# An attention and expert layer on one core: a reordered opening, and maxima transposed half a step later

## The chip, the cores and the metric

The kernel runs on 1 core of one Trainium2 chip. The metric is the device time in microseconds (us) of one execution, median of the runs shown. Five engines run side by side, each with its own in-order queue: TensorE (PE; the profile lists its weight loads as PEld), VectorE (DVE), ScalarE (ACT), GpSimd (POOL) and SyncE (SP), which only issues DMAs. ACT and POOL issue DMAs too.

## The reference, cut to what matters

`x` has 4 sequences of 2048 tokens and 512 channels; all is float32.

```python
xn = layernorm(x)
# attention: 16 heads of 32
q, k, v = split(xn @ w_qkv)                    # w_qkv: 512 x 1536
q, k = irfft(rfft(q) * sigmoid(mask_logits)), irfft(rfft(k) * sigmoid(mask_logits))   # in each head
attn = softmax(q @ k.T / sqrt(32))             # 2048 x 2048 for each head
a = concat_heads(attn @ v) @ w_out + b_out
# experts: the best of 8 for each token, 100 places in each expert, first come first served
best = argmax(softmax(xn @ w_gate))
f = gate * (xn @ w_expert + b_expert) for the tokens that have a place, else 0
out = x + a + f
```

## The kernel before, in words

**Filter.** The spectral filter of q and k is a 32 x 32 matrix for each head. It is folded into the weights: `filter_steps(c)` gives, for the column chunk c (128 columns, four heads) of the q weights (s = 0) and the k weights (s = 1), a step `turned` (four transposes on PE into a PSUM bank, a copy to SBUF) and a step `filtered` (four matmuls with the filter matrix `filt`, a copy, and for c > 0 a DMA into the DRAM scratch `wd[c]`). The unfiltered weights stand in `raw`. The filter matrix comes from the mask (`mask`, `freq`, a sigmoid on ACT, one matmul, `same_head`).

**Tokens.** `token_stage(b)` gives the steps of a sequence, for its 16 tiles of 128 tokens: `load`, `measure` (two statistics instructions on DVE), `scale` (on POOL, the last part on DVE where `shift_on` is given), `normalize` (ACT, or DVE with `fast`), `turn` (four transposes on PE, a copy on ACT into `xnT`).

**Head groups and blocks.** The work is 16 groups k (4 sequences x 4 chunks of four heads), each with 4 query blocks n of 512 queries. `projections(k)` gives the pieces that make queries, keys and values of a group; a piece covers 128 tokens (16 small matmuls and a copy on ACT), or 512 with `tiles = TQ`. `key_steps(n)` forms differences of neighbouring key tiles on POOL.

**Maxima.** The softmax needs the greatest score of each query and head before the exponentials. `stream` lists the items: 32 for each block (k, n). An item takes two matmuls (`max_matmuls`, array<-keys,q) into two of the eight PSUM banks, and a reduction of both on DVE (`max_reduce`, part<-array; one instruction of 128 x 1024 if the banks are neighbours, else two of 128 x 512). When the 32nd item of a block is reduced, the block goes to `full_blocks`; `max_negate` makes the negated maxima `neg` on DVE; `max_turn` transposes them on PE (array<-square,neg), either inside the next projection piece, in a spare part of its bank, or in a bank of its own; `max_store` copies them with ACT, `max_split` splits them into three bfloat16 rows on POOL and sends these with three DMAs to `negm`, which `shift` multiplies into the scores' banks at the start of a block.

**The main loop.** A half is one key tile j of a block: 16 halves make a block, two halves a window, 1024 halves the loop. A half holds two items of the maxima stream, the scores of the key tile (array<-q,steps_of_keys), two exponentials on ACT (even or odd <-array), the products with the values of the tile before (array<-even,v or odd,v) and their sum on DVE (num), and then the steps of its `agenda`. PE's queue is in program order, so what waits in a half holds all of PE's work behind it. `MAX_AHEAD` says how many items the stream is ahead of the loop: so many are done in the opening.

**The planner.** `plan(k)` fills the agenda. `spread` lays steps with a cost over the halves at the lowest even level at which all are placed in time; key pieces may come only after the old keys are spent (`after_keys_are_spent`, `SPENT`).

**Order.** `on.tensor`, `on.vector`, `on.scalar`, `on.gpsimd` are held in program order by `InOrder`. In the opening, DMAs on SP (`nc.sync`) are not held so; from the maxima on, `on.sync` is.

**The opening before** loads all q and k weights, then x; filters all four chunks; normalizes and turns the first four tiles; projects keys and queries of the first block in pieces of 512 columns; then takes 40 items one by one, with wide pieces at items 6, 14, 22, 28 and 33 and turns in between (`ahead`). `closing` puts a block's transposition two items after its negation. In the main loop the transposition follows the negation within the same half:

```python
while full_blocks:
    splits[window + 1] = full_blocks.pop(0)
    max_negate(*splits[window + 1])
    negated.append(splits[window + 1])
if left:
    products(*left)
...
for step in agenda[2 * window + (j == odd)]:
    step()
if negated:
    max_store(max_turn(bank(), 0))
```

Of the kernel before, what the change touches and what calls it, by code (L numbers as in the profile page):

```python
# [25 lines left out]
P = 128  # L26
# [16 lines left out]
MAX_AHEAD = 40  # L43
# [3 lines left out]
def shape_constants():  # L47
# [19 lines left out]
        "c_square": square.astype(np.float32),  # L67
        "c_falling": np.ascontiguousarray(falling, dtype=np.float32),
        "c_token": token.astype(np.float32),
# [34 lines left out]
def attention_and_top1_experts(ctx: ExitStack, tc: tile.TileContext, a: dict, out: bass.AP):  # L104
# [28 lines left out]

    mask = const.tile([2 * NF, 1], F32, name="mask")
# [5 lines left out]
    square = const.tile([P, 3, P], F32, name="square")  # L140
    nc.scalar.dma_start(out=square, in_=a["c_square"])
    ident, upto, same_head = (square[:, j, :] for j in range(3))
# [30 lines left out]
    wd = [dram1.tile([P, NR, 3, P], F32, name=f"wd{c}") for c in range(NG)]  # L173
    wg = {}
    raw = {}
    for s in range(2):
        both = probs(s == 1)
        for g in range(NR // 2):
            raw[s, g] = both[:, g]
            nc.sync.dma_start(out=raw[s, g], in_=w_qkv[:, 2 * g : 2 * g + 2, s * DM : (s + 1) * DM])  # L180
# [14 lines left out]
    def filter_steps(c):  # L195
# [3 lines left out]
        def turned(s):  # L199
            if s == 0:  # L200
                held["wt"] = probs(c % 2 == 1)
            pt = bank()
            for r in range(NR):
                on.tensor.transpose(
                    pt[:, r * P : (r + 1) * P], raw[s, r // 2][:, r % 2, c * P : (c + 1) * P], ident
                )
            on.vector.tensor_copy(held["wt"][:, s, 0, :], pt)
# [22 lines left out]
    def token_stage(b):  # L230
# [10 lines left out]
        def load_tile(i):  # L241
            n, t = divmod(i, TQ)
            if t == 0:
                held[n] = chunk("xs")
            on.sync.dma_start(out=held[n][:, t : t + 1, :], in_=x[b, n, :, t : t + 1, :])
# [163 lines left out]
    def load_qkv_weights(k, s):  # L409
        wg[k, s] = weights.tile([P, NR, P], F32, name=f"w{s}", bufs=1)  # L410
        on.sync.dma_start(out=wg[k, s], in_=wd[k % NG][:, :, s, :])
# [348 lines left out]
    load, measure, scale, normalize, turn, first_route, first_sums, _ = token_stage(0)  # L760

    load(0)
# [3 lines left out]
    for s in range(3):  # L766
        wg[0, s] = weights.tile([P, NR, P], F32, name=f"w{s}", bufs=1)
    nc.sync.dma_start(out=wg[0, 2], in_=w_qkv[:, :, 2 * DM : 2 * DM + P])
    for c in range(1, NG):
        cols = slice(2 * DM + c * P, 2 * DM + (c + 1) * P)  # L770
        nc.sync.dma_start(out=wd[c][:, :, 2, :], in_=w_qkv[:, :, cols])
    filters = [filter_steps(c) for c in range(NG)]
    turned, filtered = ([f[2 * s + i] for f in filters for s in range(2)] for i in range(2))
    for i in range(2 * NG + 1):
        if i < 2 * NG:
            turned[i]()
        if i > 0:
            filtered[i - 1]()
        if 2 * NG - TQ <= i < 2 * NG:
            measure(i - 2 * NG + TQ)  # L780
    for s in range(3):
        nc.sync.dma_start(out=wd[0][:, :, s, :], in_=wg[0, s])
    first_projections = projections(0, TQ)
# [4 lines left out]
    for i in range(TQ):  # L788
        measure(TQ + i)
    scale(TQ, 2 * TQ, on.vector)  # L790
    for i in range(TQ, 2 * TQ):
        normalize(i)
        measure(TQ + i)
    first_projections[0]()
    scale(2 * TQ, 3 * TQ, on.vector)
    for i in range(2 * TQ, 3 * TQ):
        if i == 3 * TQ - 1:
            first_projections[1]()
        normalize(i)
        measure(TQ + i)  # L800
    scale(3 * TQ, NT, on.vector)
    falling = const.tile([P, E], F32, name="falling")
    nc.scalar.dma_start(out=falling, in_=a["c_falling"])
    token = const.tile([P, NT], F32, name="token")
    nc.scalar.dma_start(out=token, in_=a["c_token"])

    w_gate = const.tile([P, NR, DH], F32, name="w_gate")
    nc.gpsimd.memset(w_gate, 0.0)
    nc.scalar.dma_start(out=w_gate[:, :, 0:E], in_=a["L0_ffn_w_gate"].rearrange("(r p) e -> p r e", p=P))
    b_out = const.tile([P, DM], F32, name="b_out")  # L810
    nc.scalar.dma_start(out=b_out, in_=a["L0_attn_b_out"].partition_broadcast(P))


# [5 lines left out]
    for table in tables:  # L819
        nc.sync.dma_start(out=table.rearrange("(t p) c -> p t c", p=P), in_=nobody)  # L820

    load_out_weights(0)

    ahead = {6: first_projections[2], 14: first_projections[3], 22: first_projections[4]}
    ahead.update({28: first_projections[5], 33: first_projections[6]})
    for i, item in ((4, 1), (8, 9), (12, 17)):
        ahead.update({item + 2 * j: lambda i=i + 2 * j: (turn(i), turn(i + 1)) for j in range(2)})
    ahead.update({4: lambda: normalize(12), 5: lambda: normalize(13)})
    ahead.update({7: lambda: normalize(14), 8: lambda: normalize(15)})
    first_projections = projections(0)[7 * TQ :]  # L830
    on.sync = InOrder(tc, nc.sync)
    key_steps(0)
    closing = {}
    for i, item in enumerate(stream[:MAX_AHEAD]):
        if i == 30:
# [3 lines left out]
        half = next(turns), next(turns)  # L839
        max_matmuls(item, half)  # L840
        max_reduce(item, half, False)
# [302 lines left out]
```

## Time and profile before

| | |
|---|---|
| median of 3 runs | 4225.1 us (4222.73 to 4227.74) |
| the profiled execution | 4220.07 us |
| its span, first to last instruction | 4218.3 us |
| busy: PE, DVE, POOL, ACT | 99%, 82%, 70%, 59% of the span |
| mean granted clock of PE | 0.998 |
| first item of the maxima on PE | 40.20 us |
| first shift matmul of the main loop | 99.14 us |
| DMA | 685.93 MB, mean 163 GB/s |

The engines' busy shares are of the whole span. PE's matmuls are pipelined and their ends are modelled, so a PE that is busy 99% need not run at its peak. Nearly all instructions carry line 84, that of the helper `InOrder`; groups are told apart by tile names. Four-byte matmuls show as two records each, transposes as one. The granted clock of PE is given as a share of full speed, by stretch.

### The profile page before, as it was taken

The page shows a single profiled execution, that of the slowest core. Times are in us where ns is not written, and L with a number is a line of the kernel's source. Part 1 is how long each engine was busy: PE and PEld are TensorE (multiplying, and loading weights), DVE is VectorE, ACT ScalarE, POOL GpSimd, SP SyncE. Part 2 cuts the span into 40 slices and gives each one's busy share as a digit, 9 for nine tenths or more (in the row PEclk, how much of TensorE's full clock was granted, in tenths as well). Part 3 has the DMA queues.
Part 4 walks back from the last instruction along what each step waited for, and adds up shares of the span by engine and source line. Part 5 has one row for each costly group of instructions (what it writes and reads, how often), then busy time and mean ns, then how long its engine had stood idle before and what let it go on. Part 6 is the DMA issues. An engine that isn't in the chain of part 4 may idle for free.

```text
span 4218.3 us, 120261 instructions
## 1 busy us (share of the span) xinstructions
PE 4166.4 (99%) x52270; PEld 1837.7 (44%) x52270; DVE 3440.0 (82%) x4962; ACT 2489.1 (59%) x3411; POOL 2968.4 (70%) x2046
## 2 busy tenths in 40 slices
PE   8999999999999999999999999999999999999998
PEld 4444444444444444444444444444444443444432
DVE  6778888987788888897788888888778888788896
ACT  3555556666565556657565556566656555556665
POOL 1567776776876767776687766767668776677873
PEclk9999999999999999999999999999999999999999
DMA  4667778997788778899677787899877976778788
GB/s 121 144 139 154 155 159 163 220 197 151 139 158 161 155 156 164 187 199 193 132 158 157 156 161 150 162 199 203 169 148 146 183 158 134 148 160 165 156 170 178
DMA packets 183416, 685.93 MB, mean 163 GB/s; under 512 B 26902, under 2 KB 56760, under 8 KB 117608
## 3 DMA queue, kind: packets, MB, share of 16 engines
q0 software_dynamic: 110432, 605.83, 73.5%
q1 hardware_dynamic: 71280, 71.90, 5.4%
q8 instruction: 409, 6.70, 0.6%
q14 instruction: 119, 0.97, 0.1%
q10 hardware_dynamic: 1176, 0.52, 0.1%
HBM read 71.85 MB, written 88.96 MB: 38 GB/s over the span
## 4 chain that ended last, share of the span: by engine, by line
PE 93%; DVE 5%; DMA 1%; issue 1%; ACT 0%; POOL 0%; SPq 0%; ACTq 0%; POOLq 0%; DVEq 0%
PE array L84 93%; DVE part L84 3%; DVE num L84 1%; DVE factor L84 0%; DMA even<-odd 0%; ACT odd L84 0%; DVE stats L84 0%; DMA w<-wd 0%; ACT even L84 0%; DMA odd<-in_L_attn_w_qkv_dram 0%; DVE even L84 0%; POOL rstd L84 0%; DVE neg L84 0%; DMA mask<-_L_attn_mask_logits_dram 0%; DVE mv L84 0%
## 5 line engine op out<-in xcount | busy, mean ns | idle before, releaser
L84 DVE TENSOR_REDUCE part<-array 128x1 f32<-128x512 f32 (+1 forms) x3132 | 2483.3, 848 | 681.0 <-PE array L84 678.0
L84 POOL TENSOR_TENSOR even<-even 128x1024 f32<-128x1024 f32 x876 | 2123.6, 2528 | 410.5 <-DMA even<-odd 406.5
L84 PE MATMUL array<-keys,q 32*128 32x512 f32 x8192 | 2066.0, 614 | 7.9 <-DVE num L84 2.9
L84 PE MATMUL array<-q,steps_of_keys 32*128 32x512 f32 x8192 | 2030.7, 616 | 2.4 <-issue 2.1
L84 ACT ACTIVATE odd<-array 128x1024 f32<-128x1024 f32 x1024 | 996.0, 1021 | 483.3 <-PE array L84 413.4
L84 ACT ACTIVATE even<-array 128x1024 f32<-128x1024 f32 x1024 | 994.2, 1021 | 447.6 <-PE array L84 434.8
L84 PEld LDWEIGHTS array<-keys,q 32*128 32x128 f32 x8192 | 776.9, 184 | 565.8 <-DVE part L84 351.1
L84 PEld LDWEIGHTS array<-q,steps_of_keys 32*128 32x128 f32 x8192 | 691.9, 184 | 274.6 <-issue 250.8
L84 POOL DMA_DIRECT2D even<-odd x510 | 464.8, 911 | 394.9 <-ACT odd L84 346.6
L84 DVE TENSOR_TENSOR num<-num,array 128x512 f32<-128x512 f32 x960 | 650.5, 678 | 23.5 <-PE array L84 23.4
L84 PEld LDWEIGHTS array<-xnT,w 128*32 128x32 f32 x15808 | 443.3, 110 | 264.0 <-DVE part L84 172.3
L84 PE MATMUL array<-even,v 128*32 128x512 f32 x4096 | 545.5, 605 | 1.0 <-DVE part L84 1.0
L84 PE MATMUL array<-odd,v 128*32 128x512 f32 x4096 | 545.9, 605 | 0.0
L84 PE MATMUL array<-xnT,w 128*32 128x128 f32 (+1 forms) x15808 | 525.2, 277 | 1.5 <-ACT xnT L84 0.7
L84 PEld LDWEIGHTS array<-w,xnT 128*32 128x32 f32 x8192 | 230.4, 110 | 146.8 <-DVE part L84 106.6
L84 DVE RECIPROCAL factor<-den 128x64 f32<-128x64 f32 x504 | 274.4, 545 | 0.0
L84 PE MATMUL array<-wo,ot 128*32 128x512 f32 x2048 | 267.0, 594 | 5.0 <-POOL ot L84 5.0
L84 PE MATMUL array<-w,xnT 128*32 128x128 f32 x8192 | 269.4, 273 | 1.3 <-DMA w<-wd 1.1
L84 PEld LDWEIGHTS array<-even,v 128*32 128x32 f32 x4096 | 80.6, 108 | 390.1 <-DVE part L84 381.2
L84 PEld LDWEIGHTS array<-odd,v 128*32 128x32 f32 x4096 | 80.8, 108 | 388.4 <-DVE part L84 379.9
L84 POOL DMA_DIRECT2D out_dram<-y x63 | 86.5, 1373 | 202.8 <-ACT y L84 125.6
L84 ACT COPY q<-array 128x128 f32<-128x128 f32 (+1 forms) x250 | 66.9, 268 | 186.1 <-PE array L84 182.3
(129 smaller groups left out, 1478.9 us busy)
## 6 DMA issues: line engine op xcount, KB each, us to landing
even<-odd POOLq DMA_DIRECT2D x510, 1024.0 KB, 8.4
out_dram<-y POOLq DMA_DIRECT2D x63, 1024.0 KB, 9.8
xs<-in_L_attn_x_dram SPq DMA_DIRECT2D x96, 256.0 KB
out_dram<-in_L_attn_x_dram SPq DMA_DIRECT2D x16, 1024.0 KB
w<-wd SPq DMA_DIRECT2D x45, 256.0 KB
wo<-in_L_attn_w_out_dram SPq DMA_DIRECT2D x16, 256.0 KB
negm<-row SPq DMA_DIRECT2D x192, 4.0 KB
xs<-in_L_attn_x_dram SPq DMA_DIRECT2D x2, 1024.0 KB
```

The lines of the kernel that those rows point to most:

```text
L84: done = act(*args, **kwargs)
```

## The change

- **Constants.** `falling` and `token` join `square` in one array, loaded first, on SP. `w_gate` and `b_out` are loaded on SP too, after x.
- **Loads.** Of the q and k weights, the first 128 columns of each are loaded first, then the first 512 tokens of x in two transfers, then the other columns, then the rest of x. `on.sync` is in order from here. The value weights are read from `w_qkv` itself, not from `wd`, which has two parts instead of three.
- **Order of the opening.** Chunk 0 is turned and filtered; four tiles measured; chunk 1 turned; four tiles normalized and turned; chunk 1 filtered; four tiles measured; five pieces of 128 tokens projected. Then 42 items follow in 21 pairs: both items' matmuls, both reductions, then the steps of `beside[p]`: turns, pieces of 128 tokens, the remaining measures and normalizations, chunks 2 and 3 (their `turned` copies on ACT), the key steps, and at pairs 14 to 17 one clearing of an expert table each, written in another layout.
- **Maxima.** `MAX_AHEAD` is 42. A negated block waits in `fresh` until the next half, where it is transposed.
- **Planner.** `spread` takes latest places, used for the key pieces: a step is not moved past its latest half to keep the level.

```diff
-MAX_AHEAD = 40
+MAX_AHEAD = 42
...
+    square = const.tile([P, 3 * P + E + NT], F32, name="square")
+    nc.sync.dma_start(out=square, in_=a["c_square"])
...
-    wd = [dram1.tile([P, NR, 3, P], F32, name=f"wd{c}") for c in range(NG)]
+    wd = [dram1.tile([P, NR, 2, P], F32, name=f"wd{c}") for c in range(NG)]
...
-        both = probs(s == 1)
-        for g in range(NR // 2):
-            raw[s, g] = both[:, g]
-            nc.sync.dma_start(out=raw[s, g], in_=w_qkv[:, 2 * g : 2 * g + 2, s * DM : (s + 1) * DM])
+        raw[s] = probs(s == 1).rearrange("p g r n -> p (g r) n")
+        nc.sync.dma_start(out=raw[s][:, :, 0:P], in_=w_qkv[:, :, s * DM : s * DM + P])
...
-            on.vector.tensor_copy(held["wt"][:, s, 0, :], pt)
+            copy = on.vector.tensor_copy if c < 2 else on.scalar.copy
+            copy(held["wt"][:, s, 0, :], pt)
...
-        on.sync.dma_start(out=wg[k, s], in_=wd[k % NG][:, :, s, :])
+        cols = slice(2 * DM + k % NG * P, 2 * DM + (k % NG + 1) * P)
+        on.sync.dma_start(out=wg[k, s], in_=w_qkv[:, :, cols] if s == 2 else wd[k % NG][:, :, s, :])
...
+    on.sync = InOrder(tc, nc.sync)
+    for i in range(0, TQ, 2):
+        load_tile(i, 2)
+    for s in range(2):
+        on.sync.dma_start(out=raw[s][:, :, P:], in_=w_qkv[:, :, s * DM + P : (s + 1) * DM])
     load(1)
     load(2, chunk("y"))
     load(3, probs(False).rearrange("p u h q -> p (u h) q"))
...
+    first_projections = projections(0)
...
+    for step in (*turned0, *filtered0):
+        step()
+    for i in range(TQ):
+        measure(i)
+    for step in turned1:
+        step()
     scale(0, TQ, on.vector)
     for i in range(TQ):
         normalize(i, fast=True)
         turn(i)
+    for step in filtered1:
+        step()
+    for i in range(TQ, 2 * TQ):
+        measure(i)
+    scale(TQ, 2 * TQ)
+    for i in range(TQ + 1):
+        project_first(i)
...
+    beside = {p: [] for p in range(MAX_AHEAD // 2)}
+    for p, pieces in enumerate(((5,), (6, 8), (7, 9), (10, 11), (12,), (13,), (14,), (15,), (16,), (17,), (18,), (19,))):
+        beside[p] += [lambda i=i: project_first(i) for i in pieces]
+    for i in range(TQ):
+        beside[i].insert(0, lambda i=i: turn(TQ + i))
+        beside[3 * TQ + i].append(lambda i=i: project_first(5 * TQ + i))
+        beside[4 * TQ + i].append(lambda i=i: project_first(6 * TQ + i))
+    for n in (1, 2):
+        for i in range(TQ // 2):
+            for t in (2 * i, 2 * i + 1):
+                beside[TQ * n + i].insert(t % 2, lambda t=t, n=n: turn((n + 1) * TQ + t))
+    for i in range(TQ):
+        beside[i // 2].append(lambda i=i: measure(3 * TQ + i))
+        beside[1 + i // 2].append(lambda i=i: normalize(2 * TQ + i))
+        beside[3 + i // 2].append(lambda i=i: normalize(3 * TQ + i))
+    beside[2].append(lambda: scale(3 * TQ, NT))
+    for p, step in zip((6, 7, 8, 9, 10, 11, 12, 13), (*turned2, *filtered2, *turned3, *filtered3)):
+        beside[p].append(step)
...
+    for p in range(MAX_AHEAD // 2):
...
+        both = [(item, (next(turns), next(turns))) for item in stream[2 * p : 2 * p + 2]]
+        for item, half in both:
+            max_matmuls(item, half)
+        for item, half in both:
+            max_reduce(item, half, False)
+        if negated:
+            first = negated[0]
+            max_store(max_turn(bank(), 0))
+            max_split(*first)
+        for step in beside[p]:
+            step()
         while full_blocks:
+            negated.append(full_blocks.pop(0))
+            max_negate(*negated[-1])
...
-                while half < first or done + cost / 2 > level * (half - base + 1):
+                stop = latest.get(place, last + 1)
+                while half < stop and (half < first or done + cost / 2 > level * (half - base + 1)):
...
+                latest[place] = start + SPENT + i // TQ * TQ + 3 * TQ - 1
...
-                    while full_blocks:
-                        splits[window + 1] = full_blocks.pop(0)
-                        max_negate(*splits[window + 1])
-                        negated.append(splits[window + 1])
+                    negated.extend(fresh)
+                    if negated:
+                        splits[window + 1] = negated[0]
+                    fresh = [full_blocks.pop(0) for _ in range(len(full_blocks))]
+                    for filled in fresh:
+                        max_negate(*filled)
```

## The prediction

> **What bounds the kernel now.** I read the page first, then the waits of TensorE, the opening by stretches, and the main loop in order of time. The page says who sets the end: PE is busy 99% of the span and carries 93% of the chain that ended last.
>
> ```profile
> PE 4166.4 (99%) x52270; PEld 1837.7 (44%) x52270; DVE 3440.0 (82%) x4962; ACT 2489.1 (59%) x3411; POOL 2968.4 (70%) x2046
> ...
> PE 93%; DVE 5%; DMA 1%; issue 1%; ACT 0%; POOL 0%; SPq 0%; ACTq 0%; POOLq 0%; DVEq 0%
> ```
>
> So an edit pays only where PE stands still or runs at a low clock. The waits of PE alone (total us, times, longest) name one wait above all, that for the negated maxima:
>
> ```profile
> PE array L84 <- DVE neg L84: 13.0, 15, 0.9
> ...
> PE array L84 <- DVE part L84: 6.2, 9, 3.5
> ```
>
> The rest lies in the opening, the first 99 us. Columns here: stretch, its length, busy time (instructions) of PE, PEld, DVE, ACT, POOL, granted clock, DMA share, GB/s.
>
> ```profile
> 28.40:33.00 4.60, 3.94 (x20) 0.99 (x24) 2.99 (x9) 2.04 (x4) 1.27 (x2) 0.50 1.07 181
> 33.00:40.20 7.20, 5.05 (x49) 1.21 (x41) 5.56 (x13) 4.81 (x9) 2.51 (x3) 1.00 0.95 43
> 40.20:95.60 55.40, 54.41 (x466) 23.43 (x467) 43.77 (x50) 14.64 (x26) 6.45 (x9) 1.00 0.05 7
> 95.60:99.10 3.50, 0.08 (x1) 0.00 (x0) 3.49 (x5) 0.00 (x0) 0.00 (x0) 0.82 0.92 318
> 99.10:104.50 5.40, 5.36 (x48) 2.72 (x51) 2.52 (x3) 2.05 (x2) 0.00 (x0) 0.50 0.49 179
> ```
>
> The maxima begin at 40.20 and the main loop at 99.10, when DVE has reduced the last of the 40 items. PE stands still for the last 3.5 us, and runs the next 5.4 us at clock 0.50. From 40.2 to 99.2 the waits of DVE hold one group, five stalls behind whole 512-column projections:
>
> ```profile
> DVE part L84 <- PE array L84: 10.1, 5, 2.4
> ```
>
> In the main loop I time a half by the starts of its product matmuls (array<-even,v or odd,v). First a half with the negation and no projection piece, then one with a piece:
>
> ```profile
> 546.79 1.07 PE L84 MATMUL array<-even,v 128*32 128x512 f32 x8
> ...
> 548.75 0.39 PE L84 MATMUL array<-square,neg 128*16 128x128 f32 x2 [0.89 <-DVE neg L84]
> ...
> 551.00 1.07 PE L84 MATMUL array<-odd,v 128*32 128x512 f32 x8
> ```
>
> ```profile
> 421.37 1.07 PE L84 MATMUL array<-even,v 128*32 128x512 f32 x8
> ...
> 423.33 0.11 PEld L84 LDWEIGHTS array<-square,neg 128*16 128x16 f32 x2 [0.29 <-DVE neg L84]
> ...
> 423.65 0.19 PEld L84 LDWEIGHTS array<-keys,q 32*128 32x128 f32 x2 [0.21 <-issue]
> ...
> 425.58 1.07 PE L84 MATMUL array<-odd,v 128*32 128x512 f32 x8
> ```
>
> Both last 4.21. A bare half (4133.56 to 4136.95) lasts 3.39; there DVE is full (reductions 2.41, num 0.67, reciprocal 0.54, less overlaps). A half with a piece (402.38 to 406.18) lasts 3.80, one with two (542.12 to 546.79) 4.67: PE-bound, so a further piece costs 0.87.
>
> **The change part by part, from the profiled execution: 4220.07 us, span 4218.3, 1.8 around it; the three runs' median is 4225.1, 5.0 more, so I subtract from the median.** A measurement tells about 0.2% (8.4 us) from no change.
>
> *Transposition a half behind.* 64 negations; one lies in the opening. 15 halves have no piece, the last of them without maxima; 48 have one. With 42 items ahead a block of 32 is full after 11 halves of 16 instead of 12, so the transposition stays in the twelfth half and the split still heads the next window: its DMAs on SP and its POOL steps do not move. Only the reduction of part (0.22 on DVE) goes a half earlier, mostly into the two-piece halves where PE is the bound. Without a piece, PE gets back up to 0.89 per half; the bare half's 3.39 is DVE's, whose room hides most of the 0.32 from the transposition's weight load to the next (423.33 to 423.65). I take 4.21 to 3.5, 14 times 0.7 = 10; ends 6 and 13 (the whole wait). With a piece, the idle before the load is 0.29 against some 0.20 before any next load, so 0.09 is wait and 0.32 stays: 48 x 0.09 = 4; ends 0 and 10. Sum 14, ends 6 and 23. Late next: DVE in bare halves.
>
> *Planner.* Its loops, followed through with 42 and the new latest places, give this: halves with one piece go from 552 to 555, bare from 414 to 410, and the four with four pieces become threes or twos; a piece moved into a bare half costs 0.41 instead of 0.87: 4 x 0.46 = 1.8. I take 1.5.
>
> *42 items.* One pair moves from the loop to the opening. In the tail a half without maxima takes about 2.7 (4143.48, 4145.78, 4148.76, 4151.18, 4154.29) against 3.39: gain 0.7. Its price is in the next sum.
>
> *New opening, up to the first pair.* The mask chain stays: its sigmoid starts at 6.08, its matmul at 7.32. Then on PE, in the new order: two turned (1.06 each at the low clock) and two filtered (1.92), to about 13.7; turned of the second column with DVE copies of 0.69, to 16.3. DVE fits four measures of 0.79 between. Shift 0.17, four normalizations 1.91, turns behind them: 19. Two filtered, 2.1 to 3.8: 21 to 23. Five pieces of 0.9 to 1 and a 0.27 copy: 26 to 28. I take 27, against 40.2. DMA covers this: it moves 340 to 400 GB/s there, first columns (0.5 MB) and the first 512 tokens of x (1 MB) need about 5 us of it, the remaining columns (1.6 MB) some 4 more, before PE wants them at 14. If that cover fails, each us late is a us. SP now issues these in program order, behind nothing but the table of constants and the first columns. The four small loads taken off ACT's queue (0.35 to 0.68 each) had no waiter, nor had the tables.
>
> *The 21 pairs.* PE: a pair 1.0 (four items 2.00 at 83.46), 12 turns x 0.51, 23 pieces x 0.93, the late filters 4 x (0.60 + 1.06), together 55. DVE: 42 x 1.22, four measures, one negation: 55. They do not overlap fully: a pair needs four of eight banks, so PE leads by one pair at most. Taking the later engine per pair: two of 4.05 (with measures), two of 3.4, two of 2.95, two of 4.03 (two turns, piece, filtered), two of 3.0, four of 2.55, seven of 2.43: 62; with the first matmuls and the waits for a new key block (ACT copies, 0.3 to 1.0 each) 65. ACT's 29 us and SP's late table clears lie beside. Ends: 57 (full overlap) and 70. So the loop starts at 27 + 65 = 92, not 99.1: gain 7; ends -2 and 14. PE then waits 2.4, not 3.5, for the last reductions, so the low clock at 99.10 (2.7 lost) may be spared: 1.3; ends 0 and 2.7.
>
> Sum: 14 + 1.5 + 0.7 + 7 + 1.3 = 24.5; 4225.1 - 24.5 = 4200.6.
>
> **Rivals.**
> *The opening gives nothing:* the late filters make the pairs as long as the earlier start saved. For it: pairs of 4.03 where PE and DVE alternate. Then 16 from the loop: 4209. Chance 0.17.
> *The wait only changes its name:* DVE, full in bare halves, holds PE as long. For it: 3.39 is DVE's. Against: 4.21 is 0.82 above it. The opening alone: 4215, 0.10. If both fail, 4225, 0.04 (with it the case that pieces still transpose in the same half).
> *Slower, the clock:* in the opening PE waits for banks in every pair and does 12 turns and four transposed weight tiles between. From 28.4 to 33 the clock was 0.50 after such a mix. If it stays there, PE's 2.6 per pair doubles to 5.3, 2.2 beyond the present 3.1; 11 of 21 pairs cancel the gain, all cost 46: 4247. Against: 40.2 to 95.6 ran at 1.00 with the same turns and bank waits up to 0.84. Chance 0.05.
> The Trainium skill ("TensorE: Matmul & The Clock Gate", section "A second HAM failure mode: psum-queue depth-cycling") says that PE idling briefly between groups while PSUM banks cycle lets the clock swing between half and full; by it this rival would be the forecast. The trace's 55 us at 1.00 disagree.
> *Narrow pieces:* six blocks go from 512 to 128 columns. A wide block takes 3.57 (59.72 to 63.29); four narrow ones at 0.87 to 0.99 take 3.5 to 4.0, which is in the sum. If narrow cost what record means suggest (273 against 638 ns, four for one: 1.7 times), 28 pieces cost 0.6 more each: 17 off, 4217. Chance 0.02.
> The same page's section "Back-to-back issue gap" gives 81 ns at 128 columns against 131 at 512, so 2.5 times; by it, as an estimate, the sum would be 35 us worse. The rows above disagree.
>
> **How the numbers follow.** Forecast 0.62. It, the quiet opening, and part of the DVE case hold the range: both gains at their good ends (opening 14 + 2.7, loop 19 of 23, planner and tail 2.5) give 4187; the opening alone at a little less than its sum gives 4217. Faster by over 0.2%: 0.62 + 0.17 + half of 0.10 + 0.01 = 0.85; within: the other half and both failing, 0.09; slower: the clock and a late DMA, 0.06.
>
> **What would show it.** Right: first maxima near 27; the first shift matmul (array<-negm,ones_b) near 92; PE <- DVE neg gone from the waits; halves with the transposition at 3.4 to 3.6 bare and about 4.1 with a piece. Wrong: clock 0.5 between 30 and 90; turned weights of the second column waiting for raw; pairs longer than 3.1 on average; bare halves still at 4.2 behind DVE part.

## The result and the profile after

| | before | after |
|---|---|---|
| median (5 runs each) | 4225.1 us (4221.72 to 4227.74) | 4203.85 us (4199.95 to 4205.65) |
| the profiled execution, its span | 4220.07, 4218.3 us | 4199.95, 4197.9 us |
| first maxima on PE | 40.20 us | 26.08 us |
| first shift matmul | 99.14 us | 92.04 us |
| first product matmul | 106.77 us | 97.73 us |

The ratio is 0.9947, with a 95% interval of 0.9934 to 0.9961. The forecast was 4200.6, its range 4187 to 4217; the change is faster by half a per cent, 21 us of the 24.5 forecast.

The first lines of the page: PE is as full as before, in a span that is 20.4 us shorter, and it still holds the chain that ended last. (In the kernel after, the helper is line 82.)

```profile
PE 4154.1 (99%) x52846; PEld 1852.0 (44%) x52846; DVE 3436.8 (82%) x4952; ACT 2493.4 (59%) x3436; POOL 2968.2 (71%) x2052
...
PE 93%; DVE 4%; DMA 1%; issue 1%; ACT 1%; POOL 0%; SPq 0%; ACTq 0%; POOLq 0%; DVEq 0%
```

The waits of PE (total us, times, longest) answer to the 13.0 us behind DVE neg. That wait is down to one of 0.3. A new one stands in the middle, eleven times 0.4 behind ScalarE's copies of keys, and a longer one behind ACT odd; neither was forecast.

```profile
PE array L82 <- DVE part L82: 9.6, 20, 2.3
...
PE array L82 <- ACT keys L82: 4.2, 11, 0.4
...
PE array L82 <- ACT odd L82: 2.6, 4, 1.9
...
PE array L82 <- DVE neg L82: 0.3, 1, 0.3
```

The windows of the opening, cut at the first maxima, the end of PE's work on them, the first shift and the first product (columns as before: length, busy PE, PEld, DVE, ACT, POOL, clock, DMA share, GB/s). The clock is 1.00 through all 21 pairs and, here, after the pause too:

```profile
26.08:89.68 63.60, 61.76 (x1002) 38.09 (x1003) 50.32 (x58) 27.53 (x59) 7.62 (x12) 1.00 0.11 30
89.68:92.04 2.36, 0.09 (x2) 0.00 (x1) 2.30 (x3) 0.00 (x0) 0.00 (x0) 1.00 1.04 397
92.04:97.73 5.69, 5.69 (x69) 2.78 (x68) 3.81 (x5) 2.75 (x4) 0.00 (x0) 1.00 0.28 108
```

DVE's waits for PE are no less in sum than before (13.1 against 10.1). But 3.8 of them lie ahead of the first reduction, and the eleven in the pairs, 9.3 in all, are their alternation, nine of them under 1 us, and not five stalls behind wide pieces:

```profile
DVE part L82 <- PE array L82: 13.1, 12, 3.8
```

In the main loop, first a half with the transposition and no piece, then one with a piece, timed as before by the starts of the products:

```profile
533.91 1.07 PE L82 MATMUL array<-even,v 128*32 128x512 f32 x8
...
534.79 0.38 PE L82 MATMUL array<-square,neg 128*16 128x128 f32 x2
535.62 0.70 PE L82 MATMUL array<-keys,q 32*128 32x512 f32 x2 [0.44 <-DVE part L82]
...
537.55 1.07 PE L82 MATMUL array<-odd,v 128*32 128x512 f32 x8
```

```profile
408.92 1.06 PE L82 MATMUL array<-even,v 128*32 128x512 f32 x8
...
410.57 0.21 PEld L82 LDWEIGHTS array<-square,neg 128*16 128x16 f32 x2
410.67 0.38 PE L82 MATMUL array<-square,neg 128*16 128x128 f32 x2
...
412.92 1.07 PE L82 MATMUL array<-odd,v 128*32 128x512 f32 x8
```

They last 3.64 and 4.00, against 4.21 each before. The transposition waits for neg no more: in the first case neg was made at 530.93, 3.9 us ahead, and in the second the weight load carries no wait at all. In the bare half PE now waits 0.44 for the reductions instead: DVE is late next, as forecast.

**Where the 20.4 us between the two spans lie** (I add up, half by half, the differences of the times from product to product):

| part | forecast | measured |
|---|---|---|
| start to first shift matmul | 7 | 7.1 |
| first shift to first product (clock at the seam) | 1.3 | 1.9 |
| halves with the transposition: between the products of tiles 10 and 11 of each block, but the last | 14 | 18.3 |
| halves of the last key pieces, groups 0 to 14 (planner) | in the 1.5 | -4.0 |
| all else in group 0 (planner) | in the 1.5 | 2.6 (2.1 of it a pause behind "issue" in the execution of before) |
| the half that loses its maxima: tiles 9 to 10 of the third block of group 15 (42 items) | 0.7 | 1.1 |
| last eight halves and the end | 0 | -2.2 |
| all else in group 15 | 0 | -2.1 |
| all else | 0 | -2.5 |

So the large parts came as forecast or better, the planner's had the wrong sign, and the end of the loop lost more than the 42 items brought there. The experiments took up both.

### The profile page after: what moved, and what is told of

It reads as the page before. It is cut to its first block, busy times and chain, and to the rows that moved or that the text cites. A ratio compares the mean times of both kernels' runs of the same rounds, so it can differ in the third digit from the quotient of the medians.

```text
span 4197.9 us, 121495 instructions
## 1 busy us (share of the span) xinstructions
PE 4154.1 (99%) x52846; PEld 1852.0 (44%) x52846; DVE 3436.8 (82%) x4952; ACT 2493.4 (59%) x3436; POOL 2968.2 (71%) x2052
## 4 chain that ended last, share of the span: by engine, by line
PE 93%; DVE 4%; DMA 1%; issue 1%; ACT 1%; POOL 0%; SPq 0%; ACTq 0%; POOLq 0%; DVEq 0%
PE array L82 93%; DVE part L82 3%; DMA even<-odd 1%; DVE num L82 1%; DVE factor L82 0%; ACT odd L82 0%; POOL even L82 0%; DMA odd<-in_L_attn_w_qkv_dram 0%; DMA w<-in_L_attn_w_qkv_dram 0%; ACT even L82 0%; POOL ot L82 0%; DVE even L82 0%; ACT keys L82 0%; ACT xs L82 0%; SPq L82 0%
## 5 line engine op out<-in xcount | busy, mean ns | idle before, releaser
L82 PEld LDWEIGHTS array<-xnT,w 128*32 128x32 f32 x16384 | 458.4, 110 | 257.5 <-DVE part L82 175.9
L82 PE MATMUL array<-xnT,w 128*32 128x128 f32 x16384 | 527.4, 273 | 1.4 <-DVE part L82 0.6
L82 ACT COPY q<-array 128x128 f32<-128x128 f32 x256 | 67.9, 265 | 181.1 <-PE array L82 177.3
```

The source lines that it names most:

```text
L82: done = act(*args, **kwargs)
```

## The experiments

The first four ran beside one another, with before at 4222.93 us (21 runs); the next four with before at 4223.19; the last four with before at 4219.93. I compare within such a set.

### 1. The transposition back in the half of its negation

```diff
-                    negated.extend(fresh)
-                    if negated:
-                        splits[window + 1] = negated[0]
-                    fresh = [full_blocks.pop(0) for _ in range(len(full_blocks))]
-                    for filled in fresh:
-                        max_negate(*filled)
+                    while full_blocks:
+                        splits[window + 1] = full_blocks.pop(0)
+                        max_negate(*splits[window + 1])
+                        negated.append(splits[window + 1])
```

> The changed kernel, but with the transposition put back into the half of its negation; opening, 42 items and planner stay. Theory (PE waits for the negation whenever its transposition follows in the same half): the waits PE <- DVE neg come back, halves with one piece and the transposition go from 4.00 back to 4.21, about 58 of them, so 12 us slower than the changed kernel, about 4216. Rival (42 items alone did it, because they move the pair of steps one half earlier, from bare halves to halves with pieces that hide the wait): under 4 us slower, about 4206, and such halves stay at 4.00.

Measured: 4220.5 us (10 runs), 0.9994 of before (0.9984 to 1.0004). Halves with one piece and the transposition took 4.21 again (41 of them), those with two 5.08. The waits of PE and PEld for neg are back:

```profile
PEld array L82 <- DVE neg L82: 25.2, 63, 1.8
...
PE array L82 <- DVE neg L82: 3.9, 5, 0.9
```

The intervals between the products of tiles 9, 10 and 11 gave up 18.2 us together (28.3 lost in the first, 10.1 won in the second, since the transposition moved from one to the other). So the half behind is worth 18 us on top of the rest of the change, more than the 12 expected, and 42 items alone do not bring it. It also says that the opening, the 42 items and the planner together, without it, come to 2.4 us between the medians; the interval leaves room for anything from 2 us lost to 7 won.

### 2. The half behind, alone, on the kernel before

```diff
-                    while full_blocks:
-                        splits[window + 1] = full_blocks.pop(0)
-                        max_negate(*splits[window + 1])
-                        negated.append(splits[window + 1])
+                    negated.extend(fresh)
+                    if negated:
+                        splits[window + 1] = negated[0]
...
```

The same lines, the other way round, in the kernel before with its 40 items and its old opening.

> The kernel before, with the transposition one half later and nothing else (40 items, old opening, old planner). Theory: the gain of the main loop alone, without any wait for a key copy: 48 halves with a piece gain 0.21, 14 bare ones about 0.6, so 18 us, about 4207; the main loop still starts near 99. Rival (the change's main-loop gain needs the 42 items): under 6 us, about 4220.

Measured: 4237.4 us (6 runs), 1.0030 of before (1.0018 to 1.0043): slower. Neither theory had that. The wait for neg is gone and halves with a piece take 4.00, but PE has a new wait, for the three rows that the split sends to negm. The waits of PE, and the timeline on SP and PE at the end of group 2:

```profile
PE array L84 <- DMA negm<-row: 14.7, 4, 5.1
```

```profile
868.52 13.05 SPq L84 DMA_DIRECT2D negm<-row  x3
...
882.79 0.61 PE L84 MATMUL array<-negm,ones_b 3*128 3x512 bf16 x4 [4.22 <-DMA negm<-row]
```

With 40 items a block is full in its twelfth half; a half behind, the transposition lies in the thirteenth, and the split heads the window after that. The first row is issued at 868.5 instead of 862.7, the others, whose splits queue on POOL behind pair sums and the key steps, at 880.2 and 881.0 instead of 868.9 and 869.8, and the next block opens at 882.79. At the ends of groups 2, 6 and 10 this costs 4.3 to 6.7 us, and 3 in group 0. At the end of group 2 it is 5.8 for a wait of 4.22, for PE's granted clock is 0.50 in the 3.2 us behind the wait (882.79 to 886.00).

### 3. The changed kernel with 40 items

```diff
-MAX_AHEAD = 42
+MAX_AHEAD = 40
```

> The changed kernel with 40 items ahead instead of 42: the last key pieces have a half more, the opening has 20 pairs. Theory (the new wait PE <- ACT keys, 11 times 0.4 us, and the doubled half in its place cost 4.6 us and come from the 42 items): that wait is gone, the four halves with four pieces are back (1.4), so 3 us faster, about 4201. Rival (42 items pay, by one half less with maxima in the tail): 1 to 3 us slower, about 4206.

Measured: 4221.63 us (10 runs), 0.9997 of before (0.9987 to 1.0006), 20 us above what I expected. The key wait went, as expected (3.6 us in the halves of the last key pieces), and the first product came at 95.33, 2.4 ahead of the changed kernel's. But the wait for negm is here too:

```profile
PE array L82 <- DMA negm<-row: 12.7, 4, 4.4
```

Experiments 2 and 3 agree: the half behind and the 42 items only pay together. I had seen that 42 keeps the split at the head of the same window, and had put no price on the other case. The price is some 20 us between the medians. In the profile 12.7 of it is the wait for negm, and 8.0 lies between the products of tiles 10 and 12: with the transposition a half later, these two intervals gain 10.6 us on the kernel before instead of 18.6.

### 4. Scores ahead of the maxima where the keys are late

```diff
+                        late = (n, j) == (NQ - 1, 7)
+                        if late:
+                            scores(k, n, j, u)
                         if mate:
...
                             max_matmuls(mate, mh)
-                        scores(k, n, j, u)
+                        if not late:
+                            scores(k, n, j, u)
```

> The changed kernel; only in the half that follows the last key pieces of a group (fourth block, eighth key tile) the scores go ahead of the maxima's matmuls on PE, so that PE has work while ACT copies the keys. Theory: the wait PE <- ACT keys goes from 4.2 us to under 1 and the halves before it from 5.13 towards 4.67: 2 to 4.5 us faster, about 4200. Rival (the maxima's matmuls lie on the path, the wait only moves into the half): no gain, 4204.

Measured: 4201.71 us (4200.18 to 4202.92), 0.9948 of before (0.9932 to 0.9965). PE <- ACT keys fell from 4.2 to 0.4, but those halves still took 5.13. The rival was right. The timeline of PE, in one such half:

```profile
581.40 1.93 PE L82 MATMUL array<-xnT,w 128*32 128x128 f32 x64
583.26 0.70 PE L82 MATMUL array<-q,steps_of_keys 32*128 32x512 f32 x2
583.71 0.70 PE L82 MATMUL array<-keys,q 32*128 32x512 f32 x2
```

Elsewhere two scores and two maxima begin within 0.02 of each other (in kernel 6, at 579.40 and 579.41) and run side by side. Here the scores go alone, and the maxima that would run beside them start 0.45 later. The wait has lost its name, not its time.

### 5. The first weights whole, ahead of x

```diff
-        nc.sync.dma_start(out=raw[s][:, :, 0:P], in_=w_qkv[:, :, s * DM : s * DM + P])
+        nc.sync.dma_start(out=raw[s], in_=w_qkv[:, :, s * DM : (s + 1) * DM])
...
-    for s in range(2):
-        on.sync.dma_start(out=raw[s][:, :, P:], in_=w_qkv[:, :, s * DM + P : (s + 1) * DM])
```

> The changed kernel, but the first two thirds of w_qkv are loaded whole (2.1 MB) ahead of x, instead of the first columns (0.5 MB), x, and the remaining columns. Theory (the order of the loads is worth what the bytes ahead of x take): x comes later by 1.6 MB at the 390 GB/s of that stretch, some 4.0 us; the four measures then end near 16 instead of 12.1 and only then the first block is normalized, while the 1.2 us that PE and DVE wait for the remaining columns go away. First maxima near 29 instead of 26.1, first shift matmul near 95, time 4.2 up at most and about 3 in the middle: 4206 to 4208. Rival (the opening is bound by the mask chain and by PE's own work, and the loads lie beside it): first maxima stay within 0.5 us of 26.1 and the time is that of the changed kernel, 4200 to 4205.

Measured: 4202.72 us (4197.57 to 4204.02), 0.9949 of before (0.9932 to 0.9965); first maxima at 26.46. The rival was right: against whole weights ahead of x, the new order of loads is worth nothing that these runs show. The timeline of PE, first of the changed kernel, then of this one, shows the exchange:

```profile
13.75 0.66 PE L82 MATMUL array<-square,odd 128*128 128x128 f32 x4 [1.17 <-DMA odd<-in_L_attn_w_qkv_dram]
15.84 3.48 PE L82 MATMUL array<-square,xs 128*128 128x128 f32 x16 [1.44 <-DVE xs L82]
```

```profile
14.44 0.60 PE L82 MATMUL array<-square,odd 128*128 128x128 f32 x4
17.76 2.03 PE L82 MATMUL array<-square,xs 128*128 128x128 f32 x16 [2.72 <-DVE xs L82]
```

PE waits for the one or for the other. The turns of x begin 1.9 later, not 4, and then run in 2.03 instead of 3.48.

### 6. The last key pieces ahead of the products

```diff
+                    ahead = (n, j) == (NQ - 1, 6)
+                    if ahead:
+                        for step in steps_now:
+                            step()
                     if left:
                         products(*left)
                     left = k, n, j, tiles[j], num
-                    for step in agenda[2 * window + (j == odd)]:
-                        step()
+                    if not ahead:
+                        for step in steps_now:
+                            step()
```

> The changed kernel, but in one half in each group (that of the last two key pieces, j = 6 of n = 3) the steps of the half are issued before the product matmuls of the tile before, not after them. Theory (in the changed kernel the maxima of the next half wait 0.39 us for ScalarE to copy the keys out): the products, 0.88 us on PE, now lie between the pieces and the maxima and cover the copy. The wait of PE for ACT keys (4.2 us, 11 times) falls under 1 us, and the halves that took 5.13 come to 4.67 together with the one before: ten times 0.46 = 4.6 us off, about 4199. Rival (as with the scores ahead of the maxima, the wait only moves): the products start later, num and the banks come later, and the same 0.4 us shows at the next matmul that needs a bank; time unchanged.

Measured: 4196.65 us (4193.28 to 4199.65), 0.9935 of before (0.9919 to 0.9952). The timeline of PE in the changed kernel, then here:

```profile
577.33 1.93 PE L82 MATMUL array<-xnT,w 128*32 128x128 f32 x64
579.64 0.70 PE L82 MATMUL array<-keys,q 32*128 32x512 f32 x2 [0.39 <-ACT keys L82]
```

```profile
576.66 1.95 PE L82 MATMUL array<-xnT,w 128*32 128x128 f32 x64
578.43 1.04 PE L82 MATMUL array<-odd,v 128*32 128x512 f32 x8
579.40 0.70 PE L82 MATMUL array<-keys,q 32*128 32x512 f32 x2
```

Now the products lie between the last piece and the maxima, and there is no wait. The halves around it are together 0.43 shorter in nine of the ten groups, and 0.43 to 0.44 in all ten in kernel 11, which is the same kernel once more. The theory was right. In experiment 4 the cover was other work that needed the same partner; here it is work that needs nobody.

### 7 and 8. The value pieces one pair later; both edits

```diff
-        beside[4 * TQ + i].append(lambda i=i: project_first(6 * TQ + i))
+        beside[4 * TQ + 1 + i].append(lambda i=i: project_first(6 * TQ + i))
```

> The changed kernel, but the four value pieces of the opening go one pair later each (pairs 17 to 20 instead of 16 to 19), so that PE has 1.08 us of work behind the last pair of maxima. Theory (PE's pause of 2.3 us before the main loop is what lowers the granted clock for about 4 us in some executions, and this is most of the difference between executions at 4200 and at 4204 to 4205): the pause shrinks to about 1.2, the clock stays 1.00 between 88 and 100 in the profile, and the timed runs lie at 4198 to 4202 without those near 4205. Rival (the low clock there follows something else, or the difference between executions arises in the tail): timed runs again from 4200 to 4205.

> The changed kernel with both edits: steps before products in the half of the last key pieces, and the value pieces of the opening one pair later. The theories add up: 4.6 from the key copies and up to 4 from the clock at the seam, 4194 to 4199 and below the changed kernel. If both rivals hold, 4200 to 4205.

Measured: 4201.48 us (4199.4 to 4202.18) for 7, 0.9948 of before (0.9931 to 0.9964), and 4199.91 (4198.2 to 4201.21) for 8, 0.9944 (0.9928 to 0.9961). The pause shrank as expected, from 2.27 to 1.32, and the clock stayed at 1.00 in both profiles. But 8 is not below 6, and lies above the 4194 to 4199 expected, so the edit brings nothing that these runs can tell. The profiles of all kernels with the new opening and 42 items say why:

| | after | 1 | 4 | 5 | 6 | 7 | 8 | 9 | 11 | 12 |
|---|---|---|---|---|---|---|---|---|---|---|
| first maxima | 26.08 | 27.69 | 28.71 | 26.46 | 26.09 | 26.77 | 26.94 | 27.45 | 27.67 | 26.23 |
| from there to the first shift | 65.96 | 65.96 | 65.96 | 65.97 | 65.96 | 65.73 | 65.73 | 65.97 | 65.96 | 65.97 |
| pause of PE before it | 2.27 | 2.27 | 2.27 | 2.27 | 2.27 | 1.32 | 1.32 | 2.27 | 2.27 | 2.27 |
| most of the pause within one clock step (below) | 1.36 | 1.23 | 2.27 | 1.57 | 1.15 | 0.88 | 0.83 | 1.21 | 2.05 | 1.56 |
| first shift to first product | 5.69 | 5.69 | 7.03 | 5.69 | 5.69 | 5.76 | 5.76 | 5.69 | 6.91 | 5.69 |

The pairs are the same to a hundredth in every execution. The low clock came in two of eight executions with the pause of 2.27, and cost 1.2 to 1.3, not the 2.7 that the prediction had as its end. The windows of kernel 11 show it:

```profile
92.00:94.00 2.00, 0.37 (x4) 0.32 (x7) 1.58 (x2) 0.00 (x0) 0.00 (x0) 0.85 1.03 397
94.00:96.00 2.00, 2.00 (x16) 1.02 (x12) 0.02 (x1) 0.00 (x0) 0.00 (x0) 0.50 0.27 95
```

Why these two? In every profile the granted clock changes only in steps of 3.41 us: each low stretch that ends within the profile lasts 3.41, 6.83 or 10.24. Where the steps lie differs between executions; counted from the nearest change, they give the fourth row of the table. In kernels 4 and 11 a single step holds 2.27 and 2.05 of the pause, and the clock falls at its end, at 94.68 and 93.41, for one step. In the others a step ends within the pause and holds at most 1.57 of it, and the clock stays. The kernel before fits too: 2.1 of its 3.5 lie in the step that ends at 97.82, where its clock falls. That leaves the limit somewhere between 1.57 and 2.05, and no run here moved the pause against the steps on purpose.

The larger part of the spread in this table is the first 26 to 29 us, where PE waits for the second column of weights; how long differs between executions (1.17 in the changed kernel, 1.24 and 1.46 in kernel 9).

The Trainium skill ("TensorE: Matmul & The Clock Gate", section "HAM oscillation — how this bites in real kernels") gives the rule that PE must not stand idle for more than about 3.4 us. The trace agrees for most executions at 2.27, but not for the two that fell to 0.50. The same page of the Trainium skill says (section "What's actually happening") that the observing window is 3413 ns long and runs freely. The trace agrees: the steps of the clock are 3.41 us long, and lie differently in each execution.

### 9 to 12. The base again, the old opening, the best version, and the end

One set: the changed kernel; the kernel before with the half behind, 42 items and the latest places, but the old opening; kernel 6 again; and kernel 6 with two pair sums of the last block on GpSimd. The edits of 10 (beside that of 2) and of 12:

```diff
-MAX_AHEAD = 40
+MAX_AHEAD = 42
...
-    def spread(steps, last):
+    def spread(steps, last, latest={}):
...
```

```diff
                 if window in pairs:
-                    pair(*pairs.pop(window))
+                    if (k, n) == (B * NG - 1, NQ - 1) and w in (2, 4):
+                        add_to(*pairs.pop(window), on.gpsimd)
+                    else:
+                        pair(*pairs.pop(window))
```

> The changed kernel itself, timed again beside the next ones. Theory (executions differ by some 6 us from each other whatever the edit): median 4201 to 4205, single executions from 4200 to 4206, as the first time. The value is the base for the two kernels beside it.

> The kernel before with the half behind, 42 items ahead and the latest places of the key pieces, but with the old opening. Theory (the parts add up: the opening is worth what it brings the first product forward, 9.0 us less 2.4 for one more pair): the loop starts near 101.5, its first product comes near 109, the halves of the main loop are those of the changed kernel (one piece with the transposition 4.00, bare 3.63), no wait for negm; time 11 us above the changed kernel, 4213 to 4216. Rival (the parts work only together, as the half behind alone did not pay with 40 items): waits for negm or banks come back in the loop and the time is over 4220.

> The kernel with the steps ahead of the products in the half of the last key pieces, timed again. Theory (ten key copies covered, 4.4 us of the loop): median 3 to 5 us under the changed kernel run beside it. Rival (the 4196.65 of the first time was the spread between executions): within 1.5 us of it.

> As the kernel before this one, and in the last block two of the seven pair sums (those of windows 0 and 2 of its eight... issued at windows 2 and 4) are added by GpSimd, which is idle there, instead of by an accumulating transfer. Theory (why the 42nd item brought nothing at the end: from 4100 to 4170 the transfers are the bound, 1 MB of pair sum per window at 205 to 219 GB/s, 5.1 us, plus 1 MB of y; DVE waits up to 4.34 us for them and holds the reciprocals, the division and the projection behind it, PE stands 1.9 and 1.8 us and falls to clock 0.65): GpSimd adds a pair in 4.7 to 5.0 us beside the transfers, the waits DVE even <- DMA and ACT odd <- DMA go, PE's 3.7 us of pauses and part of the low clock too: 3 to 6 us under the kernel before this one, 4191 to 4195. Rival (the reciprocals on DVE and the chain through factor, ot and the projection are late by themselves, or GpSimd's adds slow DVE down): no more than 1 us off, or slower.

| | median us (range) | of before (95% interval) |
|---|---|---|
| 9, the changed kernel | 4198.14 (4196.41 to 4199.83) | 0.9946 (0.9932 to 0.9959) |
| 10, with the old opening | 4204.66 (4202.97 to 4205.3) | 0.9961 (0.9946 to 0.9976) |
| 11, kernel 6 again | 4194.35 (4191.07 to 4197.48) | 0.9935 (0.9921 to 0.9948) |
| 12, with two sums on GpSimd | 4189.74 (4188.64 to 4196.64) | 0.9934 (0.9920 to 0.9947) |

**9 and 11.** Kernel 9 came out below the 4201 to 4205 expected, and the kernel before is some 3 us lower too in this set. Kernel 11 is 3.8 us under kernel 9, as the theory has it, and the halves in question give 4.2 in the profiles. The intervals overlap, but the timelines of both profiles with the edit agree.

**10.** The main loop's part of the change (half behind, 42 items, planner) brings 15.3 us by itself, the new opening 6.5 on top. The rival (over 4220) is out; the theory's distance of 11 from the changed kernel was 4.5 too large, and its 4213 to 4216 too high. Its first product came at 110.08, near the 109 expected and 11.0 behind kernel 9's, and there was no wait for negm. But its loop was 5.2 shorter than kernel 9's, in short stalls, most of them in groups 6, 11 and 15, that come and go between executions of one kernel too. Whether an earlier start makes such stalls likelier stays open.

**12.** Why does the end lose more than the 42 items bring there? The windows, in kernel 11, then 12:

```profile
4160.00:4170.00 10.00, 7.22 (x36) 1.25 (x38) 7.67 (x10) 3.10 (x4) 2.85 (x2) 0.60 1.03 213
```

```profile
4150.00:4160.00 10.00, 6.56 (x44) 1.71 (x40) 10.00 (x15) 5.38 (x6) 2.62 (x2) 0.97 0.53 107
```

In kernel 11, as in the changed kernel, the DMA share is 1.0 or above in each ten us from 4130 to 4170: a window of the main loop sends 1 MB of pair sums, at 213 GB/s 4.9 us, and such windows without maxima last little longer (halves of 2.3 to 3.1). PE runs at clock 0.60. DVE waits for a sum, and behind it stand the reciprocals that the division and the projection need. With two sums on GpSimd the share falls to 0.53 and DVE's waits for transfers in this stretch go (6.7 us to 0), as does ACT odd <- DMA (3.0 to 0). The timeline of kernel 11, with DVE, and of kernel 12, with POOL, DVE and PE:

```profile
4158.55 2.36 DVE L82 TENSOR_TENSOR even<-even 128x1024 f32<-128x1024 f32 x2 [4.33 <-DMA even<-odd]
```

```profile
4142.52 5.65 POOL L82 TENSOR_TENSOR even<-even,odd 128x1024 f32<-128x1024 f32 x2 [3.39 <-PE array L82]
...
4143.13 6.12 DVE L82 TENSOR_TENSOR even<-even 128x1024 f32<-128x1024 f32 x2
...
4152.06 2.28 DVE L82 TENSOR_TENSOR even<-even 128x1024 f32<-128x1024 f32 x2
...
4159.48 1.94 PE L82 MATMUL array<-wo,ot 128*32 128x512 f32 x8 [3.44 <-POOL ot L82]
```

So theory and rival are both half right. The last eight halves are 3.8 shorter, but the halves of group 15 ahead of them 1.4 longer: 2.4 us in all, not 3 to 6. The two adds of DVE that ran while GpSimd was adding took 6.12 instead of 2.28, and PE still waits 3.4 for the division behind the reciprocals. The other 2.2 of the 4.6 between the medians are not shown to come from the edit: the two profiles differ by 2.7 at the start alone, and by 2.8 in groups that the edit does not touch. Against the kernel before, 11 and 12 have nearly the same ratio (0.9935 and 0.9934), so the timed runs alone do not tell them apart. The Trainium skill ("SBUF — State Buffer", section "SBUF: two separate sides") says that a VectorE instruction with two SBUF inputs and a GpSimd instruction that reads SBUF lock each other out of a shared port for whole instructions. The trace agrees: GpSimd's two adds ran from 4142.52 to 4148.17, and VectorE's, begun at 4143.13, ended at 4149.25, 1.1 behind them, about the length of one add (2.28 for two). Between them the engines took turns: GpSimd's first add ended at 4144.88, VectorE's first at 4145.95.

Kernel 12 has the lowest median of all, 4189.74 us, with runs from 4188.64 to 4196.64.

## Why the prediction was right, step by step

**Transposition a half behind, 14 (ends 6 and 23): right.** 18.3 between the profiles, 18.2 when it was undone. Halves with a piece went from 4.21 to 4.00, not the 4.12 of the sum: of the weight load's idle not 0.09 but 0.21 was wait. Bare halves went to 3.63, a little above the 3.5 taken. What the step did not price is the window of the split: "with 42 items the split still heads the next window" was true, and without it the gain turns into a loss (experiments 2 and 3). The rival "the wait only changes its name" is out for this wait.

**Planner, 1.5: wrong sign.** The sum had a moved piece at 0.46 us for halves, and no look at what the moved piece makes. The 42 items and the latest places put two key pieces, the group's last, one half earlier in ten groups, directly ahead of the maxima that need these keys. Each costs 0.4 of waiting for a copy on ACT, 4.0 in all. It takes the 42 items: with 40, and the latest places kept, the wait was gone (kernel 3); the latest places alone were not run. The edit of experiment 6 took it away, and kernel 11 got 4.2 back. The rest of the term, in group 0, came out at 2.6, but 2.1 of it is one pause.

**42 items at the end, 0.7: it came, and the end lost more.** The bare half that the prediction measured (4133.56 to 4136.95, 3.39) has no maxima now and lasts 2.29 (4110.84 to 4113.13), as in every profile with 42 items and the half behind. What the prediction put at nothing is the stretch behind it. The last eight halves lost 2.2, nearly all in one half (4.93 for 2.96, between the products of tiles 10 and 11). The end is paced by transfers at a share of 1.0, and the step took the length of halves without maxima as if only PE and DVE set it. The transfers' part is shown by experiment 12, where that half took 2.36. It is not the two items that did it: the same half took 5.78 and 6.54 in kernels 2 and 3, with 40 items; the profile of the kernel before, with 2.96, was a short one.

**Opening up to the first pair, 27: right by two errors.** It was 26.08 to 28.71. The mask chain did not stay: the table load before its sigmoid waited for the logits until 3.22 instead of 4.78, though their DMAs were issued at the same times, and its matmul came at 5.59, not 7.32. That was 1.7 better; why the logits landed earlier stays open. The cover "4 us more, before PE wants them at 14" failed by 1.2 to 2.7: PE waited for the second column. So the two errors cancelled, and that the sum came within 1 to 2 us is luck in part. Experiment 5 shows that another order only moves that wait to x, and that the mask chain does not set the end by itself: its matmul came at 7.99 there, and the first maxima only 0.4 later.

**The 21 pairs, 65: right.** 65.96, at clock 1.00, in eight executions alike. By the starts of their matmuls the pairs took 2.1 to 4.5 us, against 2.4 to 4.1 in the sum. The clock rival (0.05) and the dear narrow pieces (0.02) are out: five narrow pieces took 4.67 together, 0.93 each. (The latter rival speaks of six blocks; they are seven, 28 pieces, as its sum has it.) So neither of the two rules of the Trainium skill ("TensorE: Matmul & The Clock Gate") that the prediction weighed, on PSUM banks that cycle and on the gap at 128 columns, holds here.

**The clock at the seam, 1.3 (ends 0 and 2.7): right in size.** 1.9 in the profiled pair, of which 1.2 to 1.3 is lost again in two of eight executions. Which ones, the place of the clock's steps decided, so for a single profile it is chance.

**The opening gives nothing (0.17): out**, but not by much: kernel 10 leaves it 6.5 of the 21.8 us between kernel 9 and its kernel before.

## What to carry to other kernels

A step that is moved half a stage later drags along all that is scheduled behind it: before it is moved, follow its product through every queue to its last reader, and ask how much room is left there; here two items more of work in advance, with the latest places, made the difference between 15 us won (kernel 10) and 14 lost (kernel 2), both with the old opening. When a planner moves a producer, look at which instruction comes next on the consumer's engine: put work that needs neither of them in between, since a mere exchange of the waiting instruction with its partner only hides the wait. And where an engine's work at the end is made shorter, check the transfers there first: at a DMA share of 1.0, what one half gives the next can lose.

## What was not expected of the hardware

- The accumulating transfers of 1 MB ran at 200 to 228 GB/s with a DMA share of 1.0 (4130 to 4170, in the changed kernel and kernel 11), while plain loads in the opening ran at 378 to 398 GB/s with the same share (8 to 20). A full share does not mean the same rate.
- The same pause of PE, 2.27 us, lowered the granted clock to 0.50 in two of eight executions and left it at 1.00 in six, by how the 3.41 us steps of the clock divided it.
- A low clock needs no long pause. In kernel 10 the last items came one by one behind DVE: 16 matmuls of the maxima took 5.53 us from 94.78 on, where 16 had taken 2.00 from 92.33 on. The clock fell to 0.50 at 97.36, for 10.24 us. The profile counts PE as busy in these 5.53 us, since the ends of matmuls are modelled.
- DVE's two adds of 128 x 1024 took 6.12 us beside GpSimd's adds, and 2.28 alone.
- In kernel 2 three small DMAs on SP, issued as one list, were issued over 13.05 us, as each waits for its own split on POOL.
